# Two graph layers on one core: the order of the first group's work, its loads and the checks on its inputs

## The chip, the core and the metric

The kernel runs on one NeuronCore of one Trainium2 chip. The metric is device time in microseconds, from one launch to its end, over three runs. A core has five engines that the profile names: PE (TensorE: matrix products, with PEld its weight loads), DVE (VectorE), ACT (ScalarE), POOL (GpSimd) and SP (SyncE, which here only issues DMA transfers). [...]

## The reference

`x` is 64 graphs of 256 nodes with 512 features, float32; `adj` is one 256 by 256 adjacency for all. Two pre-normalised layers are added to `x`:

```python
h = relu(layernorm(x))
# layer 0: one-head graph attention, W is 512 x 256, a is 2 x 256
H = h @ W
e = leaky_relu(H @ a[0] + (H @ a[1]).T, 0.2) + NEG * (1 - adj)
x = x + concat([softmax(e) @ H, H])
h = relu(layernorm(x))
# layer 1: eight-head attention, 64 a head, masked where adj == 0
q, k, v = (split_heads(h @ W.T + b) for W, b in ((Wq, bq), (Wk, bk), (Wv, bv)))
x = x + softmax(where(adj == 0, -inf, q @ k.T / 8)) @ v @ Wo.T + bo
```

## The kernel before

**Tiling.** A group `g` is two graphs, so there are 32 groups; each graph `b` is two tiles of 128 nodes. Everything is float32. The four 512 by 512 products of layer 1 are done as seven products of half size in place of eight (Winograd's form): `operand_sums` makes four sums of the input's quarters on POOL (tile `sums`), and `weight_sums` four sums of each weight's quarters on DVE, once.

**Order.** The order on the engines is the order in which the Python generators below are advanced; `not_sooner` and `in_order` pin an instruction behind the one before it on its engine, and a scheduler may pull unpinned ones forward. The stages of a group:

- `first_norm` (L450 to L475): LayerNorm statistics (`stats`: bn_stats `st`, bn_aggr `mv`, on DVE), `factors` (`ve`, `less` on DVE, `rstd` and again `less` on POOL), `norm` (the normalised `xn`, on ACT), `turn`, `fetch` and `put`, which turn `xn` into `hT0`. Group 0 is turned on PE (`pt`, copied by ACT). Later groups are turned by DVE in blocks of 32 (`xt`), stored to DRAM (`passed`) and loaded back (`moved`), both on SP, and copied by ACT. `xt` has one buffer, `xn` two, `moved` two.
- `first_layer` (L477 to L556): four `ph` products with `w0_sb` (W and two score columns, which DVE makes from W and `a`: the eight `prod` instructions), copied to `H`; `pn` transposes; scores `e` on ACT, DVE, ACT, DVE (times `maskT`); four `po` products; DVE adds to `x` and takes statistics; then `norm`, `turn`, `fetch`, `put` to `hT1`; last `operand_sums`.
- `project` (L580 to L650): seven products each for `pq`, `pk`, `pv`, with `kept` copies on ACT.
- attention: `scores` (`sc` on PE, exp into `p` on ACT, times mask on DVE, `ps` on POOL), `weigh` (`total`, `pr` on PE, `r`, `oT` on DVE), `outputs` (`py`). `residual` adds `b_out` to `x` on POOL.

**Start.** Once, there are also: `maskT` and the two columns `bad` from `adj` (`edge`, `pt_mask`); the loads on SP; `last_bias` (`bv_wide` on POOL, product `pb` on PE, added to `b_out` on DVE); and `judge` (L249), which decides whether a bounded form without row maxima may be used: `gram` and `square` products of wq and wk, `squares` (sums of squares on ACT, written to banks of PSUM that they share with all products, `mm`, five banks), one product `total` of ten columns `part`, a power on POOL (`norm`), some one-column steps on DVE, and the flag `wrong`, which SP and, at the end, the other engines read (L51).

The main part (L748 on) advances these: eight pieces of `norms` first, then group 0's first layer, then its projection, into which pieces of group 1's first layer (`s`), of the norms (`n`) and of `judge` are woven; from L775 on comes the repeated pattern of attention and the next group's projection.

```python
    for _ in range(8):
        next(norms)
    for piece, _ in enumerate(first_layer(0)):
        for _ in range((0, 1, 2, 2, 2, 1)[piece] if piece < 6 else 0):
            next(norms, None)
    ...
    for i, parts in enumerate("n s s n s s s s s s s s s s s nn s nn n n -".split()):
```

Of the kernel before, what the change touches and what calls it, by code (L numbers as in the profile page):

```python
# [57 lines left out]
def bounded(  # L58
# [34 lines left out]
    QH = 4  # L93
# [5 lines left out]
    big = ctx.enter_context(tc.tile_pool(name="big", bufs=2))  # L99
# [7 lines left out]
    def mm(name):  # L107
        return psum.tile([P, 512], F32, tag="turn", name=name, bufs=5)
# [28 lines left out]
    def transpose(*args):  # L137
        in_order(nc.tensor.transpose(*args))  # L138
# [18 lines left out]
    nc.sync.dma_start(w0_sb[:, :, 2:], w0.rearrange("(c p) o -> p c o", p=P))  # L157
    maskT = const.tile([P, NT, N], F32, name="maskT")
    bad = const.tile([P, 2, NT], F32, name="bad")
    adj_i = att.tile([P, NT, N], I32, tag="e", name="adj_i")  # L160
    nc.sync.dma_start(adj_i, adj.rearrange("(t p) k -> p t k", p=P))
    a_b = att.tile([P, 2, F1], F32, tag="xn", name="a_b")
    nc.sync.dma_start(
        a_b, bass.AP(tensor=a0.tensor, offset=a0.offset, ap=[[0, P], [F1, 2], [1, F1]])
    )
    prod = att.tile([P, F1], F32, tag="r", name="prod", bufs=1)
    for c in range(HP):
        for s in range(2):
            vector.scalar_tensor_tensor(
                prod, w0_sb[:, c, 2:], 1.0, a_b[:, s, :], op0=ALU.mult, op1=ALU.mult,  # L170
                accum_out=w0_sb[:, c, s : s + 1],
            )
    edge = att.tile([P, NT, N], F32, tag="e", name="edge")
    vector.tensor_scalar(edge, adj_i, 0.0, None, op0=ALU.not_equal)
    pt = mm("pt_mask").rearrange("p (k q) -> p k q", k=NT)
    for kb in range(NT):
        for t in range(NT):
            transpose(
                pt[:, kb, t * P : (t + 1) * P], edge[:, t, kb * P : (kb + 1) * P], ident
            )  # L180
    vector.tensor_copy(maskT, pt)

    vector.reduce_max(bad[:, 0, :], edge, axis=AX.X)
    vector.tensor_scalar(bad[:, 0, :], bad[:, 0, :], 0.0, None, op0=ALU.is_equal)
    vector.tensor_tensor(edge, edge, adj_i, op=ALU.not_equal)
    vector.reduce_max(bad[:, 1, :], edge, axis=AX.X)

    for g in (1, 2):
        for b in range(GB):
            load(g, b)  # L190


    W11, W12, W21, W22, T2, T3, T4 = range(7)
    T1 = W12
    w_sb = {}
    for name, src in (("q", wqT), ("k", wkT), ("v", wvT)):
        w_sb[name] = const.tile([P, 2, 7, D // 2], F32, name=f"w{name}_sb")
        for i in range(2):
            nc.sync.dma_start(
                w_sb[name][:, :, 2 * i : 2 * i + 2, :],  # L200
                src[i * D // 2 : (i + 1) * D // 2, :].rearrange("(c p) o -> p c o", p=P),
            )

    w_sb["o"] = const.tile([P, 2, 7, D // 2], F32, name="wo_sb")
    bv_col = const.tile([P, 2, 2], F32, name="bv_col")
# [2 lines left out]
    for j in range(QH):  # L208
        for half in range(2):
            nc.sync.dma_start(w_sb["o"][j * S : (j + 1) * S, half, :4, :], rows[j, half])  # L210
            nc.sync.dma_start(bv_col[j * S : (j + 1) * S, half, :], bv_rows[j, half])
    bcol = {}
    for name, src in (("q", bq), ("k", bk)):
# [3 lines left out]
    nc.sync.dma_start(  # L217
        b_out, bass.AP(tensor=bo.tensor, offset=bo.offset, ap=[[0, P], [1, D]])
    )
    rexp = const.tile([P, NT], F32, name="rexp")  # L220
    gpsimd.memset(rexp, -0.5)
    ones = const.tile([P, P], F32, name="ones")
# [9 lines left out]
    def last_bias():  # L232


        pb = mm("pb")
        b = att.tile([P, 2, 2, P], F32, tag="kept", name="bv_wide")
        for q in range(NQ):
            for half in range(2):
                gpsimd.tensor_scalar(
                    b[:, half, q, :], ones, bv_col[:, half, q : q + 1], None, op0=ALU.mult  # L240
                )
                matmul(
                    pb, b[:, half, q, :], w_sb["o"][:, half, 2 * q : 2 * q + 2, :],
                    start=(q == 0 and half == 0), stop=(q == NQ - 1 and half == 1),
                )
        vector.tensor_add(b_out, pb, b_out)


    def judge():  # L249
# [28 lines left out]
        for i in range(3):  # L278
            for n, name in enumerate(("q", "k")):
# [9 lines left out]
                    )  # L289
                yield  # L290

        def squares(col, *srcs):
            sums = small.tile([P, HP], F32, tag="sums", name=f"sums{col}", bufs=2)
            for i, src in enumerate(srcs):
                to = mm(f"squares{col}_{i}")[:, : src.free_size()]
                if len(src.shape) == 3:
                    to = to.rearrange("p (a b) -> p a b", a=src.shape[1])
                scalar.activation(to, src, AF.Square, accum_out=sums[:, i : i + 1])
            vector.reduce_sum(part[:, col : col + 1], sums[:, : len(srcs)], axis=AX.X)

        squares(3, *[w_sb["v"][:, :, i, :] for i in range(HP)])
        yield
        for i in range(2):
            squares(i, w0_sb[:, :, i])
        squares(2, *[w0_sb[:, c, 2:] for c in range(HP)])
        squares(4, bcol["q"])
        squares(5, bcol["k"])
        squares(6, bv_col)
        vector.reduce_max(part[:, 7:8], bad.rearrange("p a t -> p (a t)"), axis=AX.X)
        yield  # L310
        total = mm("total")[:, :10]
        matmul(total, ones, part, start=True, stop=True)
# [139 lines left out]
    hT0 = {}  # L452

    def first_norm(g):

        xt = {}
        mv = small.tile([P, GT, 2], F32, tag="mv", name=f"mv0_{g}")
        factors, norm, turn, fetch, put = norm_T(xt, mv, f"0_{g}", g == 0)
        for b in range(GB):
            for t in range(NT):  # L460
                xt[b * NT + t] = xs[g, b][:, t, :]
                stats(mv, xt, b * NT + t, f"0_{g}")
            factors(b)
            yield
            norm(b)
            yield
            turn(b)
            yield
        for b in range(GB):
            fetch(b)  # L470
        yield
        for b in range(GB):
            hT0[g, b] = big.tile([P, HP, N], F32, tag="hT0", name=f"hT0_{g}_{b}", bufs=1)
            put(b, hT0[g, b])
            yield  # L475

    def first_layer(g):  # L477
# [36 lines left out]
        for r in range(GT):  # L514
            b, t = divmod(r, NT)
            po = mm(f"po_{g}_{r}")[:, : F1 + 1]
            for kb in range(NT):
                matmul(
                    po, pT[b][:, kb, t * P : (t + 1) * P], H[:, b * NT + kb, 2:],
                    start=(kb == 0), stop=(kb == NT - 1),  # L520
                )
            ri = small.tile([P, 1], F32, tag="ri", name=f"ri_{g}_{r}")
            vector.reciprocal(ri, po[:, F1:])
            vector.scalar_tensor_tensor(
                xt[r][:, :F1], po[:, :F1], ri, xt[r][:, :F1], op0=ALU.mult, op1=ALU.add
            )
# [12 lines left out]
        yield  # L539
# [29 lines left out]
    turn = [0]  # L569
# [177 lines left out]

    verdict = judge()  # L748
    norms = (piece for g in range(NG) for piece in first_norm(g))
    for _ in range(8):  # L750
        next(norms)
    for piece, _ in enumerate(first_layer(0)):
        for _ in range((0, 1, 2, 2, 2, 1)[piece] if piece < 6 else 0):
            next(norms, None)
        if piece == 4:
            next(verdict)
        elif piece == 9:
            last_bias()
            next(verdict)
        elif piece == 11:  # L760
            weight_sums("q")
    residual(0)
    products, pieces = project(0), first_layer(1) if NG > 1 else iter(())
    for i, parts in enumerate("n s s n s s s s s s s s s s s nn s nn n n -".split()):
        next(products)
        if i in (1, 8, 15):
            weight_sums("kvo"[i // 7])
        for part in parts:
            if part != "-":
                next(norms if part == "n" else pieces, None)  # L770
        next(verdict, None)
# [404 lines left out]
```

## Time and profile before

| | us |
|---|---|
| three runs | 2561.52, 2562.26, 2560.50 |
| the profiled execution, whole | 2559.32 |
| its span, first to last instruction | 2557.5 |
| PE busy in it | 2506.1 |
| groups of two graphs | 32 |

The span begins with the first instruction; times of instructions below are microseconds from there. A PE matmul of 128 by 256 in float32 is two records, 0.38 us each and overlapping, 0.22 us apart when the clock is full, so one half-size product (`pq`, `pk`, `pv`: four matmuls) is eight records and 1.73 us. "PEclk" is the share of the full clock that PE was granted.

### The profile page before, as it was taken

How to read it: one execution, taken by the hardware profiler on the slowest of the kernel's cores; microseconds unless marked ns; L12 is line 12 of the kernel's file. 1: busy time of each engine (PE TensorE's matmuls, PEld its weight loads, DVE VectorE, ACT ScalarE, POOL GpSimd, SP SyncE). 2: the span in 40 equal slices, each digit the busy share in tenths (PEclk: the TensorE clock that was granted, in tenths of full speed). 3: DMA queues.
4: the chain of work that ended last, by engine and by line, in shares of the span. 5: the costliest groups of instructions: out<-in, count | busy, mean ns of one | idle time of the engine just before them, and what ended most of it. 6: DMA issues, size and time to landing. Idle time of an engine off the chain costs nothing.

```text
span 2557.5 us, 41561 instructions
## 1 busy us (share of the span) xinstructions
PE 2506.1 (98%) x16158; PEld 2033.7 (80%) x16158; DVE 1774.3 (69%) x2975; ACT 1006.0 (39%) x2015; POOL 955.8 (37%) x944
## 2 busy tenths in 40 slices
PE   6899999999999999999999999999999999999998
PEld 5778888788888888878878888888888888888876
DVE  5556677776677776677676677676777766777655
ACT  3433433433434343444344334434334334344331
POOL 2333443243443243433334433334433334432432
PEclk9999999999999999999999999999999999999999
DMA  5112323222223222223123233123232122232110
GB/s 185 44 56 75 96 78 100 81 61 81 90 85 99 69 64 91 83 92 99 59 67 99 75 100 100 50 74 100 75 99 88 61 75 91 83 99 78 37 36 34
DMA packets 129353, 205.40 MB, mean 80 GB/s; under 512 B 13952, under 2 KB 78208, under 8 KB 129152
## 3 DMA queue, kind: packets, MB, share of 16 engines
q1 hardware_dynamic: 129152, 202.69, 25.2%
q8 instruction: 129, 2.11, 0.3%
q14 instruction: 72, 0.59, 0.1%
HBM read 104.08 MB, written 98.57 MB: 79 GB/s over the span
## 4 chain that ended last, share of the span: by engine, by line
PE 97%; DVE 1%; POOL 1%; ACT 1%; DMA 0%; issue 0%; SPq 0%; DVEq 0%; ACTq 0%; POOLq 0%
PE pv L135 15%; PE pq L135 15%; PE pk L135 15%; PE py L135 15%; PE sc L135 10%; PE ph L135 9%; PE pr L135 9%; PE po L135 4%; PE total L135 3%; PE pn L138 1%; POOL ps L35 0%; DVE p L35 0%; DMA a_b<-in_L_gnn_a_dram 0%; PE pt L138 0%; PE pb L135 0%; POOL x L35 0%
## 5 line engine op out<-in xcount | busy, mean ns | idle before, releaser
L35 POOL TENSOR_TENSOR ps<-p 128x512 f32<-128x512 f32 x256 | 416.3, 1641 | 706.7 <-DVE p L35 706.7
L35 DVE TENSOR_TENSOR x<-py,x 128x256 f32<-128x256 f32 x448 | 186.6, 416 | 312.6 <-PE py L135 306.0
L35 ACT ACTIVATE p<-sc 128x512 f32<-128x512 f32 x512 | 264.3, 603 | 273.2 <-PE sc L135 273.2
L35 DVE TENSOR_TENSOR p<-p,maskT 128x1024 f32<-128x1024 f32 x256 | 334.0, 1335 | 50.2 <-ACT p L35 50.2
L35 ACT ACTIVATE xn<-x,less,rstd 128x512 f32<-128x512 f32 x256 | 195.1, 813 | 319.6 <-POOL less L35 312.9
L135 PE MATMUL sc<-q,k 64*128 64x256 f32 x2048 | 266.9, 391 | 0.0
L135 PE MATMUL py<-wo_sb,o_sums 128*128 128x256 f32 x1024 | 262.9, 380 | 2.6 <-DVE x L35 2.6
L35 DVE RECIPROCAL r<-total 128x256 f32<-128x256 f32 x128 | 224.7, 1755 | 44.6 <-PE total L135 44.6
L135 PEld LDWEIGHTS sc<-q,k 64*128 64x128 f32 x2048 | 196.3, 187 | 71.7 <-issue 52.6
L135 PE MATMUL pq<-sums,wq_sb 128*128 128x256 f32 x1024 | 238.4, 381 | 10.1 <-POOL sums L35 10.1
L135 PE MATMUL pr<-p,v 128*32 128x256 f32 x4096 | 245.5, 379 | 0.0
L135 PE MATMUL ph<-w_sb,hT 128*128 128x258 f32 x1024 | 242.2, 384 | 1.0 <-ACT hT L35 1.0
L135 PE MATMUL pv<-wv_sb,sums 128*128 128x256 f32 x1024 | 241.7, 380 | 0.0
L135 PE MATMUL pk<-sums,wk_sb 128*128 128x256 f32 x1024 | 240.2, 383 | 0.0
L35 POOL TENSOR_TENSOR rstd<-ve,rexp 128x2 f32<-128x2 f32 x128 | 91.5, 715 | 395.9 <-DVE less L35 395.9
L135 PEld LDWEIGHTS pq<-sums,wq_sb 128*128 128x128 f32 x1024 | 195.8, 192 | 36.7 <-POOL sums L35 10.5
L135 PEld LDWEIGHTS ph<-w_sb,hT 128*128 128x128 f32 x1024 | 192.3, 190 | 37.8 <-ACT p L35 9.9
L135 PEld LDWEIGHTS pk<-sums,wk_sb 128*128 128x128 f32 x1024 | 192.4, 190 | 34.7 <-issue 10.3
L135 PEld LDWEIGHTS pv<-wv_sb,sums 128*128 128x128 f32 x1024 | 195.1, 190 | 26.0
L135 PEld LDWEIGHTS py<-wo_sb,o_sums 128*128 128x128 f32 x1024 | 192.4, 191 | 28.6 <-DVE x L35 3.4
L135 PEld LDWEIGHTS pr<-p,v 128*32 128x32 f32 x4096 | 135.1, 110 | 86.2
L135 PE MATMUL py<-wo_sb,oT 128*128 128x256 f32 x768 | 197.2, 380 | 2.5 <-DVE x L35 2.5
(120 smaller groups left out, 3728.2 us busy)
## 6 DMA issues: line engine op xcount, KB each, us to landing
passed<-xt SPq DMA_DIRECT2D x124, 512.0 KB, 2.7
moved<-passed SPq DMA_DIRECT2D x496, 128.0 KB, 3.5
x<-in_x_dram SPq DMA_DIRECT2D x64, 512.0 KB, 4.6
out_dram<-x SPq DMA_DIRECT2D x64, 512.0 KB, 3.7
wq_sb<-in_L_gnn_Wq_dram SPq DMA_DIRECT2D x2, 512.0 KB, 11.2
wk_sb<-in_L_gnn_Wk_dram SPq DMA_DIRECT2D x2, 512.0 KB, 11.1
wv_sb<-in_L_gnn_Wv_dram SPq DMA_DIRECT2D x2, 512.0 KB, 12.1
wo_sb<-in_L_gnn_Wo_dram SPq DMA_DIRECT2D x8, 128.0 KB, 3.5
```

The lines of the kernel that those rows point to most:

```text
L35: instruction = getattr(self.engine, operation)(*args, **kwargs)
L135: in_order(nc.tensor.matmul(*args, **kwargs))
L138: in_order(nc.tensor.transpose(*args))
```

## The change

- The loads: `a_b` before `adj`; then wq, group 1's `x`, wk, all of wo, then the eight bits of `bv_col`, bq, bk, `b_out`; wv and group 2's `x` last. Before: `adj`, `a_b`, `x` of groups 1 and 2, wq, wk, wv, wo and `bv_col` in turns, bq, bk, `b_out`.
- The eight score columns and the mask become functions: group 0's first statistics are issued, then `score_columns`; `mask` is called at the fourth piece of `first_layer(0)`. `a_b` moves from a buffer of `xn` to the one of `ps`.
- Group 0's `first_norm` puts each half of `hT0` as soon as it is turned (half 0 before half 1's transposes), and leaves out the empty steps; `hT0` of half 1 lies in a buffer of `moved`.
- `turn(0)` of group 0's second norm moves one step later, behind `last_bias`.
- `squares` writes to one SBUF tile, `room` with tag `ps`, not to PSUM banks, each pinned in order, and is spread over more steps of `judge`; W's own squares come last.
- The weave of the projection of group 0 is new, and `last_bias` and `judge` are advanced one at a time.

```diff
-    adj_i = att.tile([P, NT, N], I32, tag="e", name="adj_i")
-    nc.sync.dma_start(adj_i, adj.rearrange("(t p) k -> p t k", p=P))
-    a_b = att.tile([P, 2, F1], F32, tag="xn", name="a_b")
+    a_b = att.tile([P, 2, F1], F32, tag="ps", name="a_b", bufs=1)
...
+    adj_i = att.tile([P, NT, N], I32, tag="e", name="adj_i")
+    nc.sync.dma_start(adj_i, adj.rearrange("(t p) k -> p t k", p=P))
+
+    def score_columns():
...
+    def mask():
...
-    for g in (1, 2):
-        for b in range(GB):
-            load(g, b)
...
+    load_weights("q", wqT)
+    load(1, 0)
+    load(1, 1)
+    load_weights("k", wkT)
...
             nc.sync.dma_start(w_sb["o"][j * S : (j + 1) * S, half, :4, :], rows[j, half])
+    for j in range(QH):
+        for half in range(2):
             nc.sync.dma_start(bv_col[j * S : (j + 1) * S, half, :], bv_rows[j, half])
...
+    load_weights("v", wvT)
+    load(2, 0)
+    load(2, 1)
...
+        room = att.tile([P, D], F32, tag="ps", name="squares", bufs=1)
+
         def squares(col, *srcs):
...
-                to = mm(f"squares{col}_{i}")[:, : src.free_size()]
+                to = room[:, : src.free_size()]
...
-                scalar.activation(to, src, AF.Square, accum_out=sums[:, i : i + 1])
+                not_sooner(
+                    scalar, "activation", to, src, AF.Square, accum_out=sums[:, i : i + 1]
+                )
+                if src.free_size() == D and i < HP - 1:
+                    yield
...
             turn(b)
             yield
+            if g == 0:
+
+                pool, tag, bufs = (big, "hT0", 1) if b == 0 else (att, "moved", 2)
+                hT0[g, b] = pool.tile([P, HP, N], F32, tag=tag, name=f"hT0_{g}_{b}", bufs=bufs)
+                put(b, hT0[g, b])
+        if g == 0:
+            return
...
-                turn(0)
-                fetch(0)
-            yield
+                if g:
+                    turn(0)
+                    fetch(0)
+            yield
+        if g == 0:
+            turn(0)
...
-    for _ in range(8):
+    for piece in range(5):
         next(norms)
+        if piece == 2:
+            score_columns()
     for piece, _ in enumerate(first_layer(0)):
-        for _ in range((0, 1, 2, 2, 2, 1)[piece] if piece < 6 else 0):
+        for _ in range((0, 2, 1, 2, 2, 1)[piece] if piece < 6 else 0):
             next(norms, None)
-        if piece == 4:
+        if piece == 3:
+            mask()
+        elif piece == 4:
             next(verdict)
         elif piece == 9:
             last_bias()
+        elif piece == 10:
             next(verdict)
...
-    for i, parts in enumerate("n s s n s s s s s s s s s s s nn s nn n n -".split()):
+    for i, parts in enumerate("n s s n s s s s s s s s s s nn nn nn s - - s".split()):
```

More of the change, by code (lines that the diff above doesn't have):

```diff
@@ L165, in bounded @@
     )
[L166 to L186, printed above, removed]
-    for g in (1, 2):
-        for b in range(GB):
-            load(g, b)
+    adj_i = att.tile([P, NT, N], I32, tag="e", name="adj_i")
+    nc.sync.dma_start(adj_i, adj.rearrange("(t p) k -> p t k", p=P))
+    def score_columns():
+        prod = att.tile([P, F1], F32, tag="r", name="prod", bufs=1)
+        for c in range(HP):
+            for s in range(2):
+                vector.scalar_tensor_tensor(
+                    prod, w0_sb[:, c, 2:], 1.0, a_b[:, s, :], op0=ALU.mult, op1=ALU.mult,
+                    accum_out=w0_sb[:, c, s : s + 1],
+                )
+    def mask():
+        edge = att.tile([P, NT, N], F32, tag="e", name="edge")
+        vector.tensor_scalar(edge, adj_i, 0.0, None, op0=ALU.not_equal)
+        pt = mm("pt_mask").rearrange("p (k q) -> p k q", k=NT)
+        for kb in range(NT):
+            for t in range(NT):
+                transpose(
+                    pt[:, kb, t * P : (t + 1) * P], edge[:, t, kb * P : (kb + 1) * P], ident
+                )
+        vector.tensor_copy(maskT, pt)
+        vector.reduce_max(bad[:, 0, :], edge, axis=AX.X)
+        vector.tensor_scalar(bad[:, 0, :], bad[:, 0, :], 0.0, None, op0=ALU.is_equal)
+        vector.tensor_tensor(edge, edge, adj_i, op=ALU.not_equal)
+        vector.reduce_max(bad[:, 1, :], edge, axis=AX.X)
     W11, W12, W21, W22, T2, T3, T4 = range(7)
@@ L195, in bounded, with load_weights @@
     w_sb = {}
-    for name, src in (("q", wqT), ("k", wkT), ("v", wvT)):
+    def load_weights(name, src):
         w_sb[name] = const.tile([P, 2, 7, D // 2], F32, name=f"w{name}_sb")
@@ L294, in squares @@
             for i, src in enumerate(srcs):
-                to = mm(f"squares{col}_{i}")[:, : src.free_size()]
+                to = room[:, : src.free_size()]
                 if len(src.shape) == 3:
                     to = to.rearrange("p (a b) -> p a b", a=src.shape[1])
-                scalar.activation(to, src, AF.Square, accum_out=sums[:, i : i + 1])
+                not_sooner(
+                    scalar, "activation", to, src, AF.Square, accum_out=sums[:, i : i + 1]
+                )
+                if src.free_size() == D and i < HP - 1:
+                    yield
             vector.reduce_sum(part[:, col : col + 1], sums[:, : len(srcs)], axis=AX.X)
-        squares(3, *[w_sb["v"][:, :, i, :] for i in range(HP)])
+        yield from squares(3, *[w_sb["v"][:, :, i, :] for i in range(HP)])
         yield
         for i in range(2):
[L304 to L308, printed above, removed]
+            yield from squares(i, w0_sb[:, :, i])
+        yield from squares(4, bcol["q"])
+        yield from squares(5, bcol["k"])
+        yield from squares(6, bv_col)
         vector.reduce_max(part[:, 7:8], bad.rearrange("p a t -> p (a t)"), axis=AX.X)
+        yield
+        yield from squares(2, *[w0_sb[:, c, 2:] for c in range(HP)])
         yield
```

## The prediction

> **What bounds the kernel now.** The page first: PE is busy for nearly the whole span.
>
> ```profile
> span 2557.5 us, 41561 instructions
> PE 2506.1 (98%) x16158; PEld 2033.7 (80%) x16158; DVE 1774.3 (69%) x2975; ACT 1006.0 (39%) x2015; POOL 955.8 (37%) x944
> ```
>
> 51.4 us of PE idleness is all that an order can win at full clock. Next, busy time by stage, cut where PE stops and starts; after the colon-pair: length, busy (count) for PE, PEld, DVE, ACT, POOL, then the clock granted to PE.
>
> ```profile
> 0.00:19.13 19.13, 1.09 (x4) 0.72 (x4) 9.64 (x40) 2.14 (x3) 2.00 (x15) 1.00 0.87 316
> ...
> 39.50:44.48 4.98, 0.04 (x1) 0.00 (x1) 4.44 (x15) 0.87 (x2) 3.25 (x8) 0.92 0.05 16
> 44.48:50.50 6.02, 6.02 (x13) 3.45 (x14) 0.00 (x0) 3.23 (x5) 0.96 (x2) 0.50 0.90 241
> ...
> 81.11:88.52 7.41, 1.89 (x10) 1.34 (x8) 3.14 (x7) 7.38 (x27) 0.00 (x0) 0.97 0.00 0
> 88.52:91.50 2.98, 2.98 (x7) 2.44 (x8) 0.62 (x4) 1.02 (x8) 0.00 (x0) 0.50 0.00 0
> ...
> 122.50:132.66 10.16, 0.05 (x1) 0.00 (x1) 1.90 (x3) 3.27 (x6) 10.05 (x10) 0.65 0.41 126
> 132.66:135.85 3.19, 3.19 (x8) 2.57 (x9) 0.00 (x0) 0.00 (x0) 2.39 (x2) 0.50 0.26 60
> ...
> 143.05:220.35 77.30, 77.30 (x539) 62.20 (x540) 54.80 (x89) 33.20 (x67) 29.46 (x29) 1.00 0.23 69
> ```
>
> From 143.05 on PE never stops, 77.30 us a group, and the edits leave that loop alone. So the change is worth what it takes off the time until PE issues group 0's first attention `total`, at 143.05. Before that PE idles about 40 us, and after each long idle stretch its clock is 0.50. PE's waits up to there say for whom:
>
> ```profile
> PE pt L138 <- ACT xn L35: 13.6, 3, 8.5
> PE pq L135 <- POOL sums L35: 10.1, 1, 10.1
> ...
> PE pk L135 <- ACT squares L35: 5.5, 1, 5.5
> ```
>
> The order of time gives the rows behind these waits (start, length, engine):
>
> ```profile
> 10.94 0.43 DVE L35 SCALAR_TENSOR_TENSOR prod<-w_sb,a_b 128x256 f32<-128x256 f32 x1 [0.77 <-DMA a_b<-in_L_gnn_a_dram]
> ...
> 42.82 1.29 DVE L35 STREAM_TRANSPOSE xt<-xn 128x512 f32<-128x512 f32 x2
> ...
> 43.61 1.52 ACT L35 ACTIVATE xn<-x,less,rstd 128x512 f32<-128x512 f32 x2 [5.53 <-DVE xt L35]
> ...
> 46.24 5.73 PE L135 MATMUL pb<-wo_sb,bv_wide 128*128 128x512 f32 x8
> ...
> 93.51 2.36 POOL L35 TENSOR_TENSOR norm<-norm,power 128x10 f32<-128x10 f32 x1 [14.17 <-DVE norm L35]
> ...
> 125.12 4.92 POOL L35 TENSOR_TENSOR x<-x,b_out 128x512 f32<-128x512 f32 x4
> 130.01 1.25 POOL L35 TENSOR_TENSOR sums<-hT 128x512 f32<-128x512 f32 x1
> ```
>
> [...]0.50 after idle stretches of 4.9, 5.5 and 10.1 us, for 3 to 7 us. [...]here a 128x512 square into PSUM took 0.618 us, an exp of the same shape into SBUF 0.656, so moving four costs at most 0.2. [...]the 0.2 KB `bv_col` loads landed in 1.6 to 2.1 us when the queue was empty.
>
> **The change, part by part.** The built program shows each engine's new order; I replay it with the durations above, on the clock of before.
>
> *A. Up to group 0's `po`* (before 35.83). `x` lands at 4.52. Two statistics to `less` took 1.97 (17.15 to 19.12), POOL's two steps 0.98: `xn` at 7.8 instead of 18.27, PE at 8.6. `a_b`, now ahead of `adj`, lands 1.84 after W's 7.88 as it did after `adj`: 9.7; `adj` keeps the old last place, 10.8. But `edge` is third among the `prod`, so DVE: two prods 9.8 to 10.8, `edge` 0.43, six prods of 0.47, one reduction 0.69: 14.75. Only then come tile 2 and 3's statistics: 1.97, POOL 0.98, two `xn` 1.55, two `H` copies that stand ahead on ACT 0.75, one `hT` copy 0.55: third `ph` at 20.7. Two `ph` and `pn`: PE at 25.3, where before it was 32.1. A new wait eats part: `e` takes the buffers of `adj_i` and `edge`, so ACT waits for DVE, which first does `xt` (after `xn`, 24.45), two statistics, the `maskT` copy, `edge` against `adj` and the reduction (six of 0.65, with small ones 28.6). Then `e` 0.8, and exp and mask in turn 2.9: `po` at 31.5. **4.3 won**; PE idles 2.6 after `gram_q`, which hides its 3.6 us.
>
> *B. `po` to group 0's first `pq`* (before 20.42). Before, PE idled 4.94, then `pt` and `pb` ran at half clock (2.0 and 5.5). Now `pb` stands ahead of `pt`. `less` is ready 5.34 after the first `po`, POOL's steps 1.0, first `bv_wide` 0.6: `pb` at 38.4, 3.2 after `po` ends (35.2). The gap is shorter than any that halved the clock; I take full clock. The third and fourth `bv_wide` stand behind POOL's second `rstd`, so `pb` ends at 42.35. But the add of `pb` into `b_out` now stands on DVE ahead of `xt`, whose reading must end before `xn` may reuse its buffer (5.53 <-DVE xt above): add 0.7, `xt` 0.65, `xn` 0.8: `pt` at 44.65, a new wait of 2.3. Two `pt` 1.25, `gram_k` 3.6, one more `pt` pair's first half 0.9: `pq` at 50.4. 18.9 instead of 20.4: **1.5 won** (half clock: -0.5; a clean hiding: +6.5). The store `passed` waits on SP behind eight `bv_col` loads and 2 MB of wv and `x`: loads land 1.35 apart, so it lands near 35, before `xt` at 43.
>
> *C. First `pk` to first `pv`* (before 81.11 to 104.61, 23.5). From `pq` to `pk` the order is the same: nothing. The squares out of PSUM let the second `pk` follow at once: 5.5 idle and 1.7 of half clock go. But `total` now stands on PE before the last `pk`. Replayed: seven `pk` (six before it), four `po`, one wait of 0.5 for a `kept`: PE reaches `total` at 95.65. DVE gets there late: it waits for the small squares behind `xn` on ACT (93.65 to 95.15, itself after POOL's `less`), adds, takes statistics, does two `xt`, the `k` add: `part` at 99.35. PE waits 3.8; `total` 0.3, `pk` 1.7: `pv` at 101.4. **3.2 won** (range 1.5 to 5: with half clock, or with DVE earlier).
>
> *D. `pv` to attention's `total`* (before 104.61 to 143.05, 38.4), still on the old clock, `pv` at 101.4. POOL's power, 2.36, starts at 100.15, and DVE's test steps wait for it with group 2's statistics and `xt` queued behind (before, other work lay between). SP too reads `wrong` before it issues `moved`: 104.7. So ACT's `xn` of group 2 (107.8 to 109.35) holds the `kept` copy behind it, and PE waits 1.7 before the fifth `pv`. PE then does `sc` and two `pq`: 120.6. The second half of `hT1` is on ACT behind `xn` (`less` at 117.4, `xn` 1.55, `kept` 0.85): done at 121.1. The gain: POOL now does `sums` ahead of `ps` and of the four adds of `b_out`, 4.92 long, so the third `pq` starts 2.65 later, 123.8 (before 132.66), and the wait of 3.2 is too short for half clock, which cost 10.46-8.62=1.8. Five `pq`: `total` at 132.4, 31.0 after `pv`. **7.5 won**.
>
> Sum: 4.3+1.5+3.2+7.5 = 16.5. The spans: 2557.5-16.5 = 2541.0. The three runs' median is 4.0 above the span, so **2545.0**.
>
> **Rivals.** *Clean* (0.09): every wait named goes whole, with its slow clock: A 4.3, B 6.5, C 5.5+1.7, D 10.1+1.8: 29.9, 2531.6. For it: the waits above. Against: the orders of DVE and SP just read. *Half clock* (0.17): gaps of 3.2, 3.8 and 3.2 halve the clock after all: 2.0+1.7+1.8 lost, 2550.5. For it: [...]before the clock fell 3.1 us after work stopped at 122.5. Against: three must all be hit. *No difference* (0.05): as half clock, and `a_b` lands no sooner and C wins nothing: 11-1.1-3.2, then further small waits at 0.1 on some thirty hand-overs, 3: 3.7, 2557.8. *Slower* (0.06): SP is the bound. `passed` sits behind 28 loads, each held until an earlier one lands; `xt` and so `pt` wait for it from 43.1 on. Each us later is a us lost; from 43.1+16.5=59.6 the kernel is slower, and at 67 it takes 2569. For it: the queue is fixed and the store is last. Against: all loads together landed by 36.55 before, and the bytes are the same.
>
> **How the numbers follow.** The main case has 0.63, its own range 2541 to 2549 (C and B's bounds). The range that holds 8 in 10 reaches to half clock and stops short of clean and slower: 2539 to 2553. Two runs of this kernel differ by up to 0.07%; 0.2%, 5.1 us, is about what tells a change from none. Faster: 0.63+0.09+0.17=0.89; same 0.05; slower 0.06.
>
> **What would show it.** In the changed profile: first `pt` near 8.6, `po` near 31.5, `pb` before `pt` with `xt` after the add of `b_out`, `pq` near 50.4; no wait of `pk` for squares but one of `total`'s near 3.8; POOL's `sums` ahead of `ps`; attention's `total` near 126.5 (143.05-16.5), then 77.30 a group as before. It is wrong if `total` comes there and the span does not follow, or if a wait stands on SP.

## The result, and the profile after

The changed kernel takes **2549.86 us** in the median of six runs (2547.17 to 2551.44) against 2561.01 of six of the kernel before (2559.60 to 2562.26). The ratio is 0.9954, its 95% interval 0.9941 to 0.9967: 11.2 us faster. I had said 2545.0 with a range of 2539 to 2553. So sign and range held, but the time is the one of the rival "half clock" (2550.5), not the one of my own case. The profiled run took 2550.3; its span is 2548.7, 8.8 less than before. That pair of executions understates the gain: before's profiled one (2559.32) was faster than its median, this one slower than its own.

The page of the changed kernel, its span and the busy time of each engine:

```profile
span 2548.7 us, 41575 instructions
...
PE 2511.1 (99%) x16158; PEld 2030.3 (80%) x16158; DVE 1776.8 (70%) x2975; ACT 1007.6 (40%) x2015; POOL 957.0 (38%) x944
```

PE has the same number of instructions as before and is busy for 5.0 us more. Its gaps shrank by 13.8 (51.4 to 37.6), but 5.0 of that came back as longer work. Most of it is clock, by an estimate: PE worked 12.2 us at clock 0.50 before and 17.1 now, and half of the difference is 2.4. Another 1.5 lie at the start. Ahead of the clock's first record (23.22 before, 18.66 now) PE also ran at half speed, though the views print 1.00 where the clock has no record: the first `pt` are 0.213 us apart in both kernels, the later ones of the changed kernel 0.109. That stretch held 5.0 us of work before and 7.9 now. PE's five longest waits up to 150 us, in all, times, longest:

```profile
PE pt L138 <- ACT xn L35: 10.8, 2, 8.4
PE pb L135 <- POOL bv_wide L35: 3.9, 2, 2.9
PE total L135 <- DVE part L35: 3.5, 1, 3.5
PE pq L135 <- POOL sums L35: 3.0, 1, 3.0
PE po L135 <- DVE e L35: 2.4, 1, 2.4
```

The wait of 10.1 for `sums` is 3.0, the one of 5.5 for `squares` is gone, and in their place stand the waits that I had worked out: `po` 2.4 (2.6 predicted), `pt` behind `pb` 2.3 (2.3), `total` 3.5 (3.8), `pq` 3.0 (3.2). Each is shorter than the gaps behind which the clock of before fell (4.94, 5.52 and 10.11). Now the stages of the changed kernel in windows of time (length, busy time of PE, PEld, DVE, ACT, POOL with counts, then the clock granted to PE, the DMA share, GB/s):

```profile
42.32:50.78 8.46, 6.15 (x14) 3.12 (x15) 1.90 (x3) 2.05 (x3) 0.53 (x1) 0.72 0.15 56
...
98.96:104.00 5.04, 5.04 (x17) 4.18 (x18) 2.47 (x16) 1.91 (x4) 1.96 (x1) 0.66 0.24 98
...
123.49:130.46 6.97, 6.97 (x25) 5.84 (x26) 3.23 (x2) 1.68 (x4) 6.97 (x5) 0.76 0.67 202
134.00:211.30 77.30, 77.30 (x539) 62.03 (x540) 54.80 (x89) 33.23 (x67) 30.71 (x30) 1.00 0.22 69
```

The first three rows lie behind the gaps of `pb` and `pt`, of `total`, and of the third `pq`; in each the granted clock is well below 1. The last one shows that the loop from attention's `total` on is what it was, 77.30 us a group. So the whole difference lies ahead of that `total`, at 134.00 against 143.05.

In the order of time (start, length, engine), the rows that answer to those shown of before:

```profile
11.36 0.43 DVE L35 SCALAR_TENSOR_TENSOR prod<-w_sb,a_b 128x256 f32<-128x256 f32 x1 [4.89 <-DMA a_b<-in_L_gnn_a_dram]
...
31.86 5.40 PE L135 MATMUL po<-H,e 128*128 128x257 f32 x16 [2.40 <-DVE e L35]
...
46.90 0.69 DVE L35 TENSOR_TENSOR b_out<-pb,b_out 128x512 f32<-128x512 f32 x1 [6.61 <-PE pb L135]
47.51 1.29 DVE L35 STREAM_TRANSPOSE xt<-xn 128x512 f32<-128x512 f32 x2
48.30 1.52 ACT L35 ACTIVATE xn<-x,less,rstd 128x512 f32<-128x512 f32 x2 [15.12 <-DVE xt L35]
...
49.17 1.82 PE L138 MATMUL pt<-ident,xn 128*128 128x128 f32 x8 [2.31 <-ACT xn L35]
...
99.61 1.96 POOL L35 TENSOR_TENSOR norm<-norm,power 128x10 f32<-128x10 f32 x1 [1.78 <-DVE norm L35]
...
120.81 1.28 POOL L35 TENSOR_TENSOR sums<-hT 128x512 f32<-128x512 f32 x1 [4.03 <-ACT hT L35]
...
123.49 7.13 PE L135 MATMUL pq<-sums,wq_sb 128*128 128x256 f32 x24 [2.99 <-POOL sums L35]
...
130.26 4.95 POOL L35 TENSOR_TENSOR x<-x,b_out 128x512 f32<-128x512 f32 x4
```

The order is as predicted: the add of `b_out` ahead of `xt` (which starts at 47.51, when the add's wait of 6.61 us for `pb` is over), `xt` ahead of `xn`, `sums` 9.4 us ahead of the adds of `b_out`. What was not predicted is the length of `po`: 5.40, where before the same sixteen records took 3.71:

```profile
35.83 3.71 PE L135 MATMUL po<-H,e 128*128 128x257 f32 x16
```

Against the checkpoints of the prediction:

| stage | before | after | won | predicted |
|---|---|---|---|---|
| A, start to `po` | 35.83 | 31.86 | 4.0 | 4.3 |
| B, `po` to first `pq` | 20.42 | 24.33 | -3.9 | 1.5 |
| C, `pq` to first `pv` | 48.36 | 45.18 | 3.2 | 3.2 |
| D, `pv` to attention's `total` | 38.44 | 32.63 | 5.8 | 7.5 |
| sum | 143.05 | 134.00 | 9.05 | 16.5 |

7.5 us are missing in this pair of profiles, 5.4 of them in B; in the medians (11.2 won of 16.5) it is 5.3.

### The profile page after: what moved, and what is told of

Read it like the earlier page. It is cut to its first block, busy times and chain, and to the rows that moved or that the text cites. A ratio compares the mean times of both kernels' runs of the same rounds, so it can differ in the third digit from the quotient of the medians.

```text
span 2548.7 us, 41575 instructions
## 1 busy us (share of the span) xinstructions
PE 2511.1 (99%) x16158; PEld 2030.3 (80%) x16158; DVE 1776.8 (70%) x2975; ACT 1007.6 (40%) x2015; POOL 957.0 (38%) x944
## 4 chain that ended last, share of the span: by engine, by line
PE 96%; DVE 1%; DMA 1%; ACT 1%; POOL 0%; issue 0%; SPq 0%; DVEq 0%; ACTq 0%
PE pv L135 15%; PE pq L135 15%; PE pk L135 15%; PE py L135 15%; PE sc L135 10%; PE ph L135 9%; PE pr L135 9%; PE po L135 4%; PE total L135 3%; PE pn L138 1%; DMA a_b<-in_L_gnn_a_dram 0%; DMA x<-in_x_dram 0%; DVE p L35 0%; POOL ps L35 0%; ACT xn L35 0%
## 6 DMA issues: line engine op xcount, KB each, us to landing
wk_sb<-in_L_gnn_Wk_dram SPq DMA_DIRECT2D x2, 512.0 KB, 13.4
```

## The experiments

The theory after the result: the missing time is PE's own work at half clock, behind gaps that I had taken to be too short for it. Its rivals: the new waits themselves cost it through other engines, or one part of the change is a loss in itself. Every kernel below is the changed one with one edit, unless it says otherwise. Each was timed together with the kernel before on the same chip; times are compared as differences to that. The changed kernel itself has two such differences, -11.2 and -11.9; gains over it below are counted from -11.9, so a gain of 0.7 or less says nothing.

| kernel | median us | before on that chip | difference | half windows in its profile |
|---|---|---|---|---|
| the changed kernel again | 2548.42 | 2560.30 | -11.9 | 4 |
| identity products in five gaps | 2544.88 | 2559.63 | -14.8 | 1 |
| add of `b_out` behind `xt` | 2547.00 | 2559.63 | -12.6 | 1 |
| add behind `xt`, identity products | 2541.49 | 2560.30 | -18.8 | 0 |
| the same, `total` two products later | 2540.88 | 2560.48 | -19.6 | 0 |
| bias's product in its old place | 2545.01 | 2559.63 | -14.6 | 5 |
| squares to PSUM | 2552.68 | 2559.63 | -7.0 | 5 |
| `total` two products later | 2546.52 | 2560.30 | -13.8 | 4 |
| `adj_i` and `edge` apart from `e` | 2548.39 | 2560.30 | -11.9 | 2 |
| old string of parts | 2554.91 | 2560.48 | -5.6 | 6 |
| before, with the new start alone | 2556.67 | 2560.48 | -3.8 | 8 |
| before, with identity products | 2555.09 | 2560.48 | -5.4 | 0 |

A half window is a stretch of 3.41 us, as the clock's records mark them off, at clock 0.50, from the clock's first record to 150 us. (The changed kernel's first profile has 5, before's has 6, two of them empty. The half speed ahead of the first record is not counted.) "Identity products" are products of the 128 by 128 identity with itself, into a PSUM bank that nothing reads; `warm(n)` issues n of them.

### Does the clock decide? The changed kernel again

No edit.

> The changed kernel itself, unaltered, in further executions. Theory ([...]a window in which PE is busy under about 0.4 halves the next one, so gaps of 2.4 to 3.5 us halve it when they fall into one window and not when they lie across two): the waits of PE in this profile are the ones of the first profile within 0.3 us, but other windows run at half clock than those at 32.3, 42.6, 49.4, 100.6 and 124.5; attention's total comes at 134.0 less 1.7 for every half window fewer; the single times spread over 3 to 5 us, in which those of the kernel before spread over 2.5. Rival (the five slow stretches belong to the order of the work): the same five windows' work at half clock, attention's total at 133.7 to 134.3.

Its waits are the same as in the first profile, `total` 3.5, `pq` 3.0, `po` 2.4, `pt` 2.3, with `pb` at 3.3 and 1.0. But attention's `total` comes at 130.98, 3.0 sooner, in the same program. Half clock lies over 39.3 to 42.7, 46.1 to 49.5, 97.3 to 100.7 and 121.2 to 124.6: four windows, and none over `po`, which takes 3.71 again (1.69 less):

```profile
30.30 3.71 PE L135 MATMUL po<-H,e 128*128 128x257 f32 x16 [2.40 <-DVE e L35]
```

The other 1.54 are `a_b`, which landed at 9.71 instead of 11.25; together 3.2. The five times spread over 2.2 us, less than I expected, and their medians in the two sets lie 0.7 apart as differences to before (-11.2, -11.9).

To see what decides it, I cut the first profile along the clock's own windows (columns as above: the first number is the length, the second PE's busy time, and the clock is the third from the end):

```profile
28.90:32.31 3.41, 1.01 (x7) 0.82 (x7) 3.28 (x9) 2.81 (x6) 0.90 (x2) 1.00 0.78 93
32.31:35.73 3.42, 3.42 (x10) 2.71 (x9) 2.05 (x7) 0.88 (x2) 0.00 (x0) 0.50 1.04 367
35.73:39.14 3.41, 1.52 (x7) 0.96 (x6) 2.79 (x12) 0.00 (x0) 0.72 (x2) 1.00 1.05 409
39.14:42.55 3.41, 1.35 (x3) 0.53 (x4) 1.08 (x4) 0.00 (x0) 3.25 (x8) 1.00 0.74 286
...
121.06:124.47 3.41, 0.98 (x5) 0.88 (x6) 3.41 (x5) 1.64 (x4) 3.33 (x3) 1.00 0.36 132
124.47:127.89 3.42, 3.42 (x10) 2.70 (x9) 2.25 (x2) 0.84 (x2) 3.42 (x3) 0.50 0.65 182
```

A window with 1.01 us of work (0.30 of it) is followed by one at 0.50; 1.52 (0.45) is not, 0.98 (0.29) is. The length is the one that the trace shows: the stretches at half clock up to 150 us last 6.83, 3.41 and 10.24 us in the profile of before and 3.41 five times in this one. Where the windows begin differed between two executions of this program: the clock's first record is at 18.66 and at 15.40 us. And the window ahead of a fall was not always idle, as the 1.01 and 0.98 us show. I counted PE's busy share in every window of all fourteen profiles, from the clock's first record to 150 us; the border of "about 0.4" was on record ahead of eight of them. Of the windows under 0.40, 38 of 38 are followed by half clock (7 of them were at half clock themselves); from 0.40 to 0.48, 4 of 10; and of those that ran at full clock and were busy for 0.48 or more, none. So, by an estimate from these counts, a gap that halved the next 3.41 us had about 2 us inside one window (0.6 of 3.41), and that cost 1.7 us where PE had work for all of it: `po`'s 5.40 less 3.71. Gaps of 2.4 to 3.5 us did so or not: `po`'s 2.40 did in the first profile of this program and did not in the second, where the windows lay otherwise.

Not all of the 1.7 reaches the end. C and D together took 77.8 in both profiles of the changed kernel, each with two half windows there; in the three below that have none there (identity products in five gaps, the add behind `xt`, and both) they took 76.4. That is 1.4 for two windows, not 3.4: at full clock a wait of 1.2 for `kept_v` comes back.

### Taking the half clock away

```diff
+            if g == r == 0:
+                warm(9)                      # 128x128 products of ident
             po = mm(f"po_{g}_{r}")[:, : F1 + 1]
...
+        warm(11)
         pb = mm("pb")
```

The same goes ahead of `pb`'s third product (3), of the `pt` behind it (8), of `total` (13) and of the third `pq` (11).

> The changed kernel with 128x128 products of the identity put on PE into an unused PSUM bank, in the five gaps that it still has (9 before the first po, 11 before pb and 3 in its middle, 8 before the next pt, 13 before total, 11 before the third pq of group 1; 0.22 us each at full clock, so 2.0, 2.4, 0.7, 1.8, 2.9 and 2.4 us, each shorter than the gap's 2.4, 2.9, 1.0, 2.3, 3.5 and 3.0 of idleness). Nothing that the kernel needs is changed. Theory (the missing 7.5 us are PE's own work at half clock in the window after a gap, 1.7 us for each of five windows): the clock stays 1.00 from 9 us to 143 us, po takes 3.7 instead of 5.4, gram_k 3.7 instead of 4.7, the five pq 5.4 instead of 7.1, attention's total comes 6 to 8 us sooner (126 to 128 instead of 134.0), and the kernel takes 2542 to 2544. Rival (the waits on the other engines are the loss, whatever the clock): attention's total stays at 133 to 135 and the kernel at 2549 to 2551.

2544.88, a difference of -14.8 to the kernel before, where the changed kernel has -11.9: 2.9 us gained, less than the theory wanted. In its profile one window, 35.9 to 39.3, is still busy for 0.46 only, since eleven products ahead of `pb` and three inside it were too few, and the next one, in which `pb` runs, is at half clock. The slower `pb` then moves the add, `xt`, `xn` and `pt` with it: B took 22.26. The `pq` behind `sums` do run at full speed. Attention's `total` is at 128.69 instead of 134.00, of which 1.8 is `a_b`, which landed at 9.45. So the direction was right and the size too large.

### The add that holds `pt`

```diff
-        vector.tensor_add(b_out, pb, b_out)
+        after(vector.tensor_add(b_out, pb, b_out), turned_last[-1])   # the last xt
...
+            turned_last.append(vector.last)
```

> The changed kernel with the add of pb into b_out put behind group 1's second xt on DVE; nothing else moves. Theory (the add, waiting for pb ahead of xt, holds xt, so xn, so pt; the wait of 2.31 us of pt goes, and with it the half clock after it): first pq at 52 to 54 instead of 56.2, the kernel 2.3 to 4 us faster, 2546 to 2547.5. Rival (xn would have waited for less or the store of xt at the same time anyway): pt keeps a wait of about 2 us, 2549 to 2551.

In the profiled run the wait went as the theory said: `pt`'s wait behind `pb` is gone (its 8.5 are the start's), the first `pq` is at 50.75 (even sooner than expected), and the run took 2543.08. But it was the fastest of five; the others took 2545.45 to 2547.83, and the median's gain over the changed kernel is 0.75, no more than that kernel's own two differences lie apart. The mean clock is 0.999 in the fastest and 0.996 in the four: 0.003 of 2541 us is 7.6 us of clock, what four or five half windows take (roughly, since the means are rounded to 0.001). The profiled run kept full clock behind three gaps that lost it in the first profile of the changed kernel, those of `po`, `total` and the third `pq`. Each lay across two windows: PE was busy for 0.41 and 0.56 of them at `total`, for 0.68 and 0.45 at `pq`, and `po`'s 2.4 fell into 0.8 and 1.6, an estimate from the same windows and the end of `po` at 35.9. The windows of that run around `total`'s wait of 3.50 us:

```profile
88.61:92.02 3.41, 1.41 (x7) 0.91 (x5) 2.46 (x12) 2.96 (x15) 0.62 (x1) 1.00 0.00 0
92.02:95.44 3.42, 1.92 (x10) 1.77 (x11) 1.48 (x4) 2.51 (x7) 1.55 (x3) 1.00 0.38 153
95.44:98.85 3.41, 3.41 (x18) 3.00 (x17) 2.59 (x16) 1.42 (x3) 0.68 (x1) 1.00 0.00 0
```

Which windows ran at half clock in the other four runs is not on record, so why the median shows so little of the gain stays partly open. The next pair closes the argument from the other side.

> The changed kernel with the add of pb behind xt on DVE and identity products in the four gaps that are left (9 before po, 13 and 4 around pb's first half, 13 before total, 11 before the third pq of group 1). Theory (what is left of the loss is the clock): no half window between 20 and 145 us, attention's total at 125 to 127.5, the time 2541 to 2543.5 in every execution with a spread under 2 us plus what the landing of a_b adds (it landed at 9.4 or at 11.3 in the profiles so far). Rival (the identity products delay what stands behind them as much as the clock gives): 2544 to 2547, as the add alone.

With the add moved and identity products in the four gaps left (9, 13 and 4, 13, 11), there is no half window in the profile, the mean clock is 0.999 or 1.000 in all five runs, attention's `total` is at 124.81, and the time is **2541.49** (2540.81 to 2542.52): 6.9 us more off than the changed kernel. Alone the two edits gave 0.75 and 2.9. Between the two kernels with identity products the moved add makes 4.1 us, which fits its 2.3 and the half window that the other still had; without identity products it made 0.75. PE's waits there, without the start's 8.6 of `pt`:

```profile
PE pb L135 <- POOL bv_wide L35: 1.4, 2, 1.0
PE pv L135 <- ACT kept_v L35: 1.2, 1, 1.2
PE pq L135 <- POOL sums L35: 0.7, 2, 0.5
PE total L135 <- DVE part L35: 0.6, 1, 0.6
PE po L135 <- DVE e L35: 0.4, 1, 0.4
```

The identity products make no other engine sooner (`po` still starts 6.57 us after `pn`, as in the first profile); they only keep PE busy meanwhile. So what came back is PE's clock. The wait of `pv` (1.2) is the 1.7 of the prediction's part D, which the first profile hid under a slow `pv`.

The kernel before, treated alike, says how much of the change's gain the clock alone is worth:

```diff
+                if name == "1_0":
+                    warm(21 if b == 0 else 4)
                 for t in tiles:
...
+            if g == 0 and name == "k":
+                warm(23)
             second = blocks(mm(f"p{name}2_{g}"))
...
+            if g == 1 and name == "q":
+                warm(42)
             product(first, 6, False)
```

> The kernel before with identity products in its gaps (21 before group 0's pt behind po, 4 before the pt behind gram_k, 23 before the second pk, 42 before the third pq of group 1: 4.6, 0.9, 5.1 and 9.2 us in gaps of 4.9, 0, 5.5 and 10.1). Theory (before ran 0.77, 1.00, 0.87 and 0.94 of a 3.41 us window at half clock, each costing half its busy time: 6.1 us): no half window from 25 us on, the kernel 4 to 6 us faster, 2554 to 2556, so that about half of what the change won is to be had without any of it. Rival (half clock there is beside other waits, which take its place): at most 1 us faster.

2555.09, 5.4 us faster, with no half window in the profile. That is nearly half of what the change won, with no order changed. With both at full clock from its first record on, the new order (and the add behind `xt`) is worth 18.8 less 5.4, 13.4 us. In that stand up to 1.7 us of the half speed ahead of the first record, by an estimate: before's sixteen `pt` lie on the path to `po`, and each is 0.104 slower there.

### One part undone, or one alone

*The start alone.* The kernel before, with the changed kernel's loads, `score_columns`, `mask` and first pieces:

```diff
-    for _ in range(8):
+    for piece in range(5):
         next(norms)
+        if piece == 2:
+            score_columns()
...
+        if piece == 3:
+            mask()
```

> The kernel before with the first part of the change alone: statistics ahead of masks and score columns, and the loads in the order of use; the bias's product, gram_k, the squares in PSUM, total and the string of parts as before. Theory (A's gain goes through one for one): po starts 3 to 5.5 us sooner than 35.83 (with a_b's landing), from po to attention's total as before (107.2), the kernel 3 to 5 us faster than before. Rival (a later wait takes it back, since xt's stores and the loads of weights come when they come): from po to attention's total 110 or more, the kernel at most 1 us faster.

3.8 us faster, at the middle of what A should give; `po` starts at 30.67, `e`'s new wait is 2.4, and from `po` to attention's `total` it takes 109.9 instead of 107.2. Here too a window busy for 0.30 ahead of `po` is followed by half clock over it (`po` takes 5.39). So A gains 5.2 in this profile, and 2.7 is given back (0.7 in B, 1.4 in C, 0.7 in D). That can be the clock: PE worked 18.3 us in half windows here, 12.2 before, and half of the difference is 3.1, an estimate.

*The old string of parts:*

```diff
-    for i, parts in enumerate("n s s n s s s s s s s s s s nn nn nn s - - s".split()):
+    for i, parts in enumerate("n s s n s s s s s s s s s s s nn s nn n n -".split()):
```

> The changed kernel with the old string of parts between group 0's products, so that POOL takes the sums of group 1 behind ps and the adds of b_out again; PE's order is the same. Theory (the 5.8 us that D won came from POOL's sums being ahead): the third pq waits 8 to 10 us again and the pq behind it run at half clock, D at 37 to 39 instead of 32.6, the kernel 5 to 7 us slower than the changed one, 2553 to 2555. Rival (D's gain came from what total and the squares no longer hold): D at 33 to 34, 2548 to 2550.

6.3 us slower than the changed kernel, as the theory said. PE's order is the same; POOL's is not, and with the string DVE and ACT take some pieces in another order too. The rows of POOL and the wait of PE, in the order of time:

```profile
118.42 1.27 POOL L35 TENSOR_TENSOR ps<-p 128x512 f32<-128x512 f32 x1 [2.56 <-DVE p L35]
119.65 2.48 POOL L35 TENSOR_TENSOR x<-x,b_out 128x512 f32<-128x512 f32 x2
122.09 1.26 POOL L35 TENSOR_TENSOR sums<-hT 128x512 f32<-128x512 f32 x1
...
125.84 7.69 PE L135 MATMUL pq<-sums,wq_sb 128*128 128x256 f32 x24 [9.19 <-POOL sums L35]
```

The `sums` are behind `ps` and two adds again, the third `pq` waits 9.2 for them, and D takes 38.95.

*The squares in PSUM:*

```diff
-                to = room[:, : src.free_size()]
+                to = mm(f"squares{col}_{i}")[:, : src.free_size()]
```

> The changed kernel with the squares of the norm written to PSUM again, as before; all else as changed. Theory (the 3.2 us that C won came from freeing the PSUM bank that pk waited for): a wait of pk for squares returns, C grows from 45.2 back towards 48, the kernel takes 2552 to 2554. Rival (the squares are now handed out one at a time between the products, which alone spares pk the wait): no wait of pk for squares over 1 us, 2549 to 2551.

4.9 us slower than the changed kernel, as much as the theory wanted, but by another way. No `pk` waits for squares, as the rival said: handed out one at a time, they cost one wait of 1.8. C even takes 43.94. The loss is in D, 37.97:

```profile
92.61 1.14 PE L135 MATMUL po<-H,e 128*128 128x257 f32 x4 [1.83 <-ACT squares L35]
...
108.41 3.68 PE L135 MATMUL pv<-wv_sb,sums 128*128 128x256 f32 x8 [3.19 <-ACT kept_v L35]
```

With this edit the scheduler also put DVE's reductions and statistics in another order, so it is not the PSUM bank alone that was undone. What this shows is that the edit as a whole costs 4.9 us; that the freed bank is what C won is not shown.

*The bias's product in its old place*, `pt` first, then `pb` and `gram_k`:

```diff
         elif piece == 9:
             last_bias()
-        elif piece == 10:
             next(verdict)
```

(and `turn(0)` of group 0 back into the branch `r == 3`).

> The changed kernel with the bias's product and gram_k back in their old place on PE (pt of group 0 first, then pb, gram_k, as in the kernel before), all else as changed. Theory (moving pb moved one gap and made two; what B lost against before is po at half clock, 1.7, and the gap before pt, 2.3): a gap of 4 to 6 us between po and pt, pt and pb at half clock, first pq at 54 to 56, 2547.5 to 2550. Rival (pb ahead of pt is itself what cost B its 3.9 us): first pq at 52.3, 20.4 us after po starts, 2546.

2545.01: 2.7 us *faster* than the changed kernel. The rival's time, though its mechanism was not seen whole: B took 21.83, not 20.4, in the profiled run (the slowest of five, 2549.03; the others 2544.16 to 2545.06).

```profile
32.07 3.71 PE L135 MATMUL po<-H,e 128*128 128x257 f32 x16 [2.40 <-DVE e L35]
42.37 1.97 PE L138 MATMUL pt<-ident,xn 128*128 128x128 f32 x8 [6.60 <-ACT xn L35]
44.13 5.49 PE L135 MATMUL pb<-wo_sb,bv_wide 128*128 128x512 f32 x8
```

One gap of 6.6 us, with two slow windows behind it (41.13 to 47.95, clock 0.50), stands where the changed kernel has three of 2.9, 1.0 and 2.3, 6.2 in all. So putting `pb` into the gap hardly shortened it: the add of its result then stood ahead of `xt` on DVE, and what `pb` had filled came back behind it. That is the order. The 2.7 themselves are, as far as single executions tell, the clock: the profiled one of this kernel, with five half windows, is 10.6 below the kernel before on its chip, and the first profiled one of the changed kernel, with five too, 10.7. The four faster ones have mean clocks of 0.997 and 0.998, the profiled one 0.996. One gap offers the clock fewer chances than three; that this is why is not shown.

The four parts, each from its own run: start 3.8, string 6.3, squares 4.9, bias -2.7. Their sum is 12.3; the whole is 11.9.

*`adj_i` and `edge` in the buffers of `kept`:*

```diff
-    adj_i = att.tile([P, NT, N], I32, tag="e", name="adj_i")
+    adj_i = att.tile([P, NT, N], I32, tag="kept", name="adj_i")
...
-        edge = att.tile([P, NT, N], F32, tag="e", name="edge")
+        edge = att.tile([P, NT, N], F32, tag="kept", name="edge")
```

> The changed kernel with adj_i and edge in the buffers of kept, so that e no longer waits on ACT for DVE's last reads of them. Theory (po waits 2.4 us for e, and e for adj_i and edge): no wait of e on DVE at its start, po starts 1.5 to 2.4 us sooner after pn (6.6 in the changed kernel, 4.2 to 5 here), the kernel 1.5 to 4 us faster than the changed one, the more where the clock stays full behind the shorter gap. Rival (e is then held on DVE behind statistics and masks just as long): po still 6 us or more after pn, no gain over 0.5.

`po` starts 5.73 after `pn` instead of 6.57, 0.8 sooner where the theory wanted 1.5 to 2.4, and the time is the same (-11.9; the profiled run was the fastest of five, 2544.78). The wait moved one step on: POOL now makes all four `bv_wide` behind its second `rstd`, and `pb` waits 5.0 for them in one piece (PE's waits):

```profile
PE pb L135 <- POOL bv_wide L35: 5.0, 1, 5.0
...
PE po L135 <- POOL less L35: 1.6, 1, 1.6
```

*`total` two products later:*

```diff
+        yield
+        yield
         total = mm("total")[:, :10]
```

> The changed kernel with total and what follows from it two products later (behind the last pk and the first pv). Theory (total stands on PE 3.5 us ahead of the sums that it waits for, and holds pk and pv that wait for nothing): no wait of total over 0.5, pv from the first pk on at 18 to 19 us instead of 20.3, attention's total 3.5 to 5 us sooner, the kernel 3 to 5 us faster than the changed one on the same chip. Rival (the wait only moves: the norm comes later, so DVE's test steps and the transfers of group 2 behind them hold the third pq longer): the wait of the third pq grows from 3.0 to 6 or more, gain under 1 us.

1.9 us, half of what the theory wanted. The wait of 3.5 is gone, and two others, 1.5 and 1.1, have come (in the order of time):

```profile
97.76 1.99 PE L135 MATMUL pv<-wv_sb,hT 128*128 128x256 f32 x8 [1.48 <-DVE k L35]
...
109.69 1.99 PE L135 MATMUL pv<-wv_sb,sums 128*128 128x256 f32 x8 [1.08 <-DVE v L35]
```

The rival's growth of the third `pq`'s wait is not there: 3.1.

*All that helped, together:* the add behind `xt`, `total` two products later, identity products before `po`, around `pb` and before the third `pq`.

> The kernel of the add behind xt with identity products (before po, around pb, before the third pq), and total two products later in place of the identity products before it. Theory (total's wait of 3.5 goes and pv's of 1.5 and 1.1 come): 0.5 to 2 us faster than with total in its place, 2539.5 to 2541. Rival (DVE's k is what pv waits for either way): equal within 0.4, 2541 to 2542.

**2540.88** (2540.24 to 2541.48), ratio to before 0.9921, interval 0.9908 to 0.9935: faster than both kernels. Over the same kernel with `total` in its place it gains 0.8 as differences to before, at the low end of what was expected. From the landing of `a_b` to attention's `total` the two profiles differ by more, 113.0 against 115.0, but `a_b` landed 1.3 later in this one.

## Why the prediction was right, and where it was wrong

**The frame held.** The time until attention's `total` fell by 9.05, the span by 8.8, and the loop did not move.

**A: right, by two errors that met.** `po` was predicted at 31.5 and came at 31.86. `a_b`, which I had at 9.7, landed at 11.25 in the first profile (W, ahead of it in the queue, at 9.31 instead of 7.88); with `a_b` at 9.71, as in the second, `po` starts at 30.30. So my replay of the chain from `a_b` to `po` was 1.2 too long. I did not take that apart further. The clock of 1.00 that my first stretch shows stands for no record; PE's half speed there did not matter after the change, since the third `ph` starts 10.0 us after `a_b` lands in both profiles, with the first record at 18.66 in one and 15.40 in the other.

**B: wrong, and this is the step that failed.** "The gap is shorter than any that halved the clock; I take full clock." The shortest gap in the profile of before that had halved it was 4.9, and I used it as a bound, though it was only the smallest example. In the first profile `po` (1.7) and two windows over `pb`, `pt` and `gram_k` (3.4) ran at half clock behind gaps of 2.4, 2.9 and 2.3. With that, 18.9 becomes 24.0. `pb`'s second matmul waited 1.0 for POOL, which made `pb` some 0.8 longer than the 3.95 that I had for it: 24.8. Of that, 0.36 came off again, as the slow `po` shortened the wait behind it (2.92, and 3.28 in the second profile): 24.4, where 24.33 was measured. The new waits themselves were right. Two half windows in the second profile give 22.86.

**C: right**, 3.2, with `total` and its wait where they were predicted. The half window that I had not taken cost little here: with none, C takes 44.79, 3.6 won. Whether the freed bank or the handing out of the squares one at a time brought it stayed open.

**D: right in the order, wrong in the clock, too large by 1.7.** "The wait of 3.2 is too short for half clock": it was 3.0, the window behind it ran at 0.50, and 24 records of `pq` took 7.13, where 24 of `pv` at full clock took 5.34. The first `pv` were slow too (4.92 for 16 records, 3.72 before), but that lay where I had put a wait of 1.7 for `kept`. With no half window in it (the add behind `xt`, identity products) D takes 31.59: 6.9 won. So 1.0 of the missing 1.7 is the clock; where the other 0.6 lie stays open.

**The rivals.** Half clock, 0.17, was the case that happened. Its price came out (2550.5, measured 2549.86 and 2548.42), but partly by luck: I had 2.0 for B, 1.7 for C and 1.8 for D, where the runs point to some 4.7, 0.4 and 1.0. And I had held it unlikely, since "three must all be hit". But the chance of each was large, by an estimate from the 2 us and the 3.41 us found above: a gap of 3 us has 2 us in one window unless a border falls into its middle 1 us, which 0.29 of all positions (1 of 3.41) do, if all are equally likely. And there were five gaps, not three: `po`'s 2.4 and `pt`'s 2.3 belonged on the list. The slower rival did not happen: no wait on PE stands on SP. Its store `passed` did land at 40.85, not near 35; nothing waited for it, until the add was moved out of `xt`'s way: then `xt` waited 1.63 us for it.

## What to carry to other kernels

In these runs a gap on PE could cost twice: once as idleness, and again as up to 1.7 us of half speed (`po`: 5.40 against 3.71), where some 2 us of it fell into one of the clock's windows of 3.41 us. One long gap can therefore be cheaper than several middling ones (argued from this count, not shown alone), and a change that splits a gap has to be priced with the clock. Where a gap can't be closed, products of no use that end before the awaited operand can keep the clock: they gained 5.4 us on the kernel before, and some 7 with one reordering on the one after, with no half window left in either profile. And look at what the moved instruction's result is read by: the add behind `pb`, one line, stood ahead of the transposes on DVE, and what moving the product had filled came back as a wait of 2.3 us and a third gap for the clock.

## What the runs showed of the hardware that I had not expected

- The clock fell after windows that were only partly idle: in these fourteen profiles after every one under 0.40 busy (38 of 38), after none at 0.48 or more at full clock, in between after 4 of 10. Ends of matmuls are modelled in these records, so the border may be sharper than it looks.
- A half-clock window with PE busy for 0.63 to 0.81 of it was followed by another at half clock in five cases, and one with 0.80 to 1.00 by full clock in all others. In work done at half speed these are 0.31 to 0.40 and 0.40 or more: about the same border.
- The load of `a_b`, fourth in an unchanged queue, landed at 9.2 to 11.5 us in the twelve profiles that have it there, and at 11.25 and 9.71 in two executions of the same program. What hangs on it, up to `po`, moved along: 31.86 and 30.30.
